# Routed experts: the last three of 39 token blocks put under a condition on the number of blocks the routing fills

## The chip, the cores and the metric

The kernel runs on one core of a Trainium2 chip. The metric is device time in microseconds (us) of that core, as the median of repeated runs; lower is better. One further execution was taken under the hardware profiler, and all views of a profile in this document come from such an execution.

A core has five engines with a queue of instructions each: TensorE (PE in the views; PEld is its weight load), VectorE (DVE), ScalarE (ACT), GpSimd (POOL) and SyncE (SP, which here issues most DMAs). A name with a q behind it (SPq, POOLq) means the sequencer of that engine: register, semaphore, branch and DMA-issuing instructions. Each engine works its own queue in order and waits on semaphores for the others.

## The reference, cut to what matters

Four layers act on x, of shape 32 x 128 x 256, each as `x = x + layer(layernorm(x))`: an attention over a context, a quantized feed-forward, a second attention, and a routed feed-forward with 8 experts. The change lies in the last one:

```python
def _L1_ffn_ref(x, W1, b1, W2, b2, Wr, br):
    E, D, H = (8, 256, 1024)
    routing_logits = x @ Wr + br
    indices = jnp.argmax(softmax(routing_logits), axis=-1)
    out = jnp.zeros_like(x)
    for i in range(E):
        mask = (indices == i).astype(x.dtype)[..., None]
        h = jax.nn.relu((x * mask) @ W1[i] + b1[i])
        out = out + (h @ W2[i] + b2[i])
    return out
```

Each of the 4096 tokens meets the two weight matrices of one expert only; what the seven others add for a masked row is a constant vector for each expert (`kacc` in the kernel).

## The kernel before

The first three layers, and the counting of the routing, are done by line 1480; the change does not touch them. While the second attention is finished, each token is given an expert and a slot, and its row (layer norm and residual side by side, 2 x 256 numbers) is written to `rows_d` in DRAM.

The expert stage follows. Tokens of one expert are cut into blocks of 128 rows. The number of blocks of an expert is its count divided by 128, rounded up, at least 1 (`nblk_f`, L1510); a running sum over the experts gives where each one ends (`endb`, L1512), so that its last entry is the number of blocks in use. Since the routing is not known when the program is built, the loop is written out for the most that 4096 tokens and 8 experts can need: `NB` = 39 blocks. A block `j` past the end takes the last expert (`eb` is cut at 7) and has row numbers out of range, so that its gather and its scatter move nothing; its arithmetic is done all the same.

The order of work is not that of `j`. The blocks are laid in `NW` = 3 parts, and turn `s` takes block `SEQ[s]`: the parts are worked in rotation, each with a set of weight buffers of its own (`w1s`, `w2s`, `kbs`, indexed by `s % NW`). So a new expert's weights are fetched into one set while the two other parts are at work. Whether a part changes expert at block `j` is the flag `new`, computed on the chip; SP loads flag and expert number into registers (L1598, L1599) and issues the three weight DMAs with the flag as condition (L1600, L1606, L1609). The first set is fetched much earlier, during the second attention.

For each turn `s`:

- `fetch(s)` (L1577, POOL): gather of the 128 rows by the token numbers `tok_i`, into one of `NX` = 4 buffers `xb`, issued three turns ahead;
- `turn(s)` (L1620 PE, L1622 DVE): the 128 x 256 block is transposed;
- `inner(s)` (L1633 PE, then L1642 ACT and L1646 DVE): 1024 hidden values, bias and relu;
- `outer(s)` (L1657 PE, L1653 and L1662 DVE): back to 256 values, and the constants and the residual added;
- scatter of the rows to the output (L1663, POOL), each one waiting for the one before it to have landed;
- `fetch_1(s + 3)` and `fetch_2(s + 3)` (SP): the weights of the turn that uses this set next.

In the loop PE and DVE keep the order in which the program is written (`manual_schedule`); a scheduler orders the other three. The loop runs `inner(s)`, `turn(s + 1)`, `outer(s)`, so PE has the next transposes and products in its queue while ACT and DVE finish the hidden values. After the last turn come the closing semaphores and drains (L1743).

Of the kernel before, what the change touches and what calls it, by code (L numbers as in the profile page):

```python
# [10 lines left out]
I32 = mybir.dt.int32  # L11
# [4 lines left out]
ALU = mybir.AluOpType  # L16
# [4 lines left out]
P = 128  # L21
# [15 lines left out]
def tile_xattn_ffn_d2(  # L37
# [25 lines left out]
    nc = tc.nc  # L63
    B, S, D = x.shape
# [8 lines left out]
    E = b2.shape[0]  # L73
# [3 lines left out]
    NB = (B * S - E) // P + E  # L77

    NW = 3
    NB = -(-NB // NW) * NW  # L80
    SEQ = [(s % NW) * (NB // NW) + s // NW for s in range(NB)]

    dram = ctx.enter_context(tc.tile_pool(name="dram", bufs=1, space=DRAM))
    x1_d = dram.tile([B, P, D], F32, name="x1_d")
# [109 lines left out]
    with (  # L194
# [35 lines left out]
        def whole(parts):  # L230
# [12 lines left out]
            out=bmask8, in_=bmask8, pattern=[[-HD0, hpc]], compare_op=ALU.is_ge,  # L243
# [3 lines left out]
            out=bmask8, in_=bmask8, pattern=[[HD0, hpc]], compare_op=ALU.is_ge,  # L247
# [98 lines left out]
        def turn(b):  # L346

            t = tiles[b]
            t["tr"] = ptr.tile([P, 4, P], F32, tag="tr", name="tr")
            for k in range(KD):  # L350
                ks = slice(k * P, (k + 1) * P)
                nc.tensor.transpose(t["tr"][:, k, :], t["xn"][:, ks], ident)
                nc.tensor.transpose(t["tr"][:, KD + k, :], of(b, "c")[:, ks], ident)
# [828 lines left out]
    with (  # L1182
# [77 lines left out]
        out=below, in_=ones, pattern=[[1, P]], compare_op=ALU.is_gt,  # L1260
# [19 lines left out]
    NP, NX = 1, 4  # L1280
    W1N = w1b.shape[1]
    w1s = [res.tile([P, W1N], F32, name=f"w1s{i}") for i in range(NP)]
    w2s = [res.tile([P, MF * D], F32, name=f"w2s{i}") for i in range(NP)]
    kbs = [res.tile([P, D], F32, name=f"kb{i}") for i in range(NP)]
    xbs = [res.tile([P, W], F32, name=f"xb{i}") for i in range(NX)]
# [42 lines left out]
    with tc.manual_schedule(engines=by_hand):  # L1328
# [15 lines left out]
        for n in range(N):  # L1344
# [117 lines left out]
            out=toks, in_=toks_d.rearrange("(k c p) o -> c k (p o)", p=P, c=P)  # L1462
# [19 lines left out]
    with (  # L1482
# [28 lines left out]
        endb = dr.tile([P, E], F32, name="endb")  # L1511
# [13 lines left out]
        for s in range(NW):  # L1525
            nc.vector.memset(new[:, SEQ[s] : SEQ[s] + 1], 1.0 if s else 0.0)

        plan1 = dr.tile([P, 2], I32, name="plan1")
        plan = dr.tile([P, 2, NB], I32, name="plan")
        for i, v in enumerate((eb, new)):  # L1530
            nc.vector.tensor_copy(plan1[:, i : i + 1], v[:, SEQ[1] : SEQ[1] + 1])

        def plan_others():
            for i, v in enumerate((eb, new)):
                nc.vector.tensor_copy(plan[:, i, :], v)
# [40 lines left out]
        def gather(dst, table, idx, bound):  # L1576
            nc.gpsimd.indirect_dma_start(  # L1577
                out=dst, out_offset=None, in_=table,
                in_offset=bass.IndirectOffsetOnAxis(ap=idx, axis=0),
                bounds_check=bound, oob_is_err=False,  # L1580
            )
# [3 lines left out]
        def fetch(s):  # L1585
            j = SEQ[s]
            gather(xbs[s % NX], rows_d, tok_i[:, j : j + 1], B * P - 1)

        exps_, news = {}, {}

        def fetch_1(s):

            j = SEQ[s]
            row = (
                [plan1[0:1, i : i + 1] for i in range(2)] if s == 1
                else [plan[0:1, i, j : j + 1] for i in range(2)]
            )
            exps_[s] = nc.sync.value_load(row[0], min_val=0, max_val=E - 1)  # L1598
            news[s] = nc.sync.value_load(row[1], min_val=0, max_val=1)  # L1599
            nc.sync.dma_start(  # L1600
                out=w1s[s % NW], in_=w1b[bass.ds(exps_[s] * P, P), :], cond=news[s] > 0
            )

        def fetch_2(s):
            e, new_ = exps_.pop(s), news.pop(s)
            nc.sync.dma_start(  # L1606
                out=w2s[s % NW], in_=w2[bass.ds(e * P, P), :], cond=new_ > 0
            )
            nc.sync.dma_start(  # L1609
                out=kbs[s % NW],  # L1610
                in_=kacc_d[bass.ds(e, 1), :].rearrange("e d -> (e d)").partition_broadcast(P),
                cond=new_ > 0,
            )
# [9 lines left out]
            return xbT  # L1623

        def inner(j, xbT):
            wb = w1s[j % NW]
            hT = wk_.tile([P, MF, P], F32, tag="hT", name="hT")
            for q in range(2):
                h_ps = ph.tile([P, 4, P], F32, tag="h", name="h_ps")
                for c4 in range(4):  # L1630
                    c = q * 4 + c4
                    for k in range(KD):
                        nc.tensor.matmul(  # L1633
                            h_ps[:, c4, :],
                            lhsT=wb[:, k * FF + c * P : k * FF + (c + 1) * P],
                            rhs=xbT[:, k, :], start=(k == 0), stop=(k == KD - 1),
                        )
                for c4 in range(4):
                    c = q * 4 + c4
                    b1c = wb[:, KD * FF + c : KD * FF + c + 1]  # L1640
                    if c4 < 2:
                        nc.scalar.activation(  # L1642
                            hT[:, c, :], h_ps[:, c4, :], AF.Relu, bias=b1c
                        )
                    else:
                        nc.vector.tensor_scalar(  # L1646
                            hT[:, c, :], h_ps[:, c4, :], b1c, 0.0, ALU.add, ALU.max
                        )
            return hT

        def outer(j, hT):
            xk = wk_.tile([P, D], F32, tag="xk", name="xk")
            nc.vector.tensor_tensor(xk, xbs[j % NX][:, :D], kbs[j % NW], ALU.add)  # L1653
            w2t = w2s[j % NW].rearrange("p (c d) -> p c d", d=D)
            y_ps = py.tile([P, 512], F32, tag="y", name="y_d")
            for c in range(MF):
                nc.tensor.matmul(  # L1657
                    y_ps[:, :D], lhsT=hT[:, c, :], rhs=w2t[:, c, :],
                    start=(c == 0), stop=(c == MF - 1),
                )  # L1660
            yb = wk_.tile([P, D], F32, tag="yb", name="yb")
            nc.vector.tensor_tensor(yb, y_ps[:, :D], xk, ALU.add)  # L1662
            nc.gpsimd.indirect_dma_start(  # L1663
                out=out_rows, out_offset=bass.IndirectOffsetOnAxis(
                    ap=tok_i[:, SEQ[j] : SEQ[j] + 1], axis=0
                ),
                in_=yb, in_offset=None, bounds_check=B * P - 1, oob_is_err=False,
            )


        with tc.manual_schedule(engines={mybir.EngineType.PE, mybir.EngineType.DVE}):
            for s in range(NX - 1):
                fetch(s)
            fetch_1(1)
            fetch_2(1)
            nxt = turn(0)
            plan_others()
            fetch_1(2)
            fetch_2(2)
            for s in range(NB):  # L1680
                hT = inner(s, nxt)
                if s + NW < NB:
                    fetch_1(s + NW)
                if s + 1 < NB:
                    nxt = turn(s + 1)
                if s + NX - 1 < NB:
                    fetch(s + NX - 1)
                outer(s, hT)
                if s + NW < NB:
                    fetch_2(s + NW)  # L1690


# [54 lines left out]
```

## Time and profile before

| | us |
|---|---|
| median of 3 runs | 1617.8 (1615.79 to 1618.09) |
| the profiled execution, its own time | 1616.39 |
| its span, first to last instruction | 1614.7 |
| busy PE / PEld | 1521.8 / 1132.9 |
| busy DVE / ACT / POOL | 950.5 / 809.0 / 461.1 |
| mean granted TensorE clock | 0.988 of full |
| products L1633 and L1657 of the 39 blocks, busy | 147.8 + 141.1 |
| first product of the expert stage, last scatter issued | 1318.58, 1604.00 |

Times of instructions are counted from the start of the span. A row of a group gives line, engine, operation, tiles and count, then busy time and the mean of one in ns, then idle time of the engine just before and what ended it. A row of one line of the source gives the durations of its instructions as min/median/max in ns, and when the first and the last began. A row of a stretch gives its length, the busy time of each engine with the number of instructions, the granted clock, the share of time in which the DMA engines were busy, and what they moved in GB/s.

### The profile page before, as it was taken

How to read it: one execution, taken by the hardware profiler on the slowest of the kernel's cores; microseconds unless marked ns; L12 is line 12 of the kernel's file. 1: busy time of each engine (PE TensorE's matmuls, PEld its weight loads, DVE VectorE, ACT ScalarE, POOL GpSimd, SP SyncE). 2: the span in 40 equal slices, each digit the busy share in tenths (PEclk: the TensorE clock that was granted, in tenths of full speed). 3: DMA queues.
4: the chain of work that ended last, by engine and by line, in shares of the span. 5: the costliest groups of instructions: out<-in, count | busy, mean ns of one | idle time of the engine just before them, and what ended most of it. 6: DMA issues, size and time to landing. Idle time of an engine off the chain costs nothing. (4 is left out here: it accounts for less than half of the span.)

```text
span 1614.7 us, 28238 instructions
## 1 busy us (share of the span) xinstructions
PE 1521.8 (94%) x10062; PEld 1132.9 (70%) x10062; DVE 950.5 (59%) x2275; ACT 809.0 (50%) x2421; POOL 461.1 (29%) x533
## 2 busy tenths in 40 slices
PE   7999998999988899999999999999999969999997
PEld 4665665544433588787777777777777649999996
DVE  6989896347999434465555566566655433333332
ACT  5787885447979432655555555554455401111111
POOL 6566663000000002233333333323332222232321
PEclk9999999999999999999999999999999979999998
DMA  7222211002438756122111110010000343134410
GB/s 230 86 67 77 69 38 50 0 33 85 160 148 263 239 184 229 36 49 84 56 55 53 53 53 27 27 27 21 9 14 14 92 164 105 53 105 160 154 35 8
DMA packets 83724, 137.76 MB, mean 85 GB/s; under 512 B 13034, under 2 KB 61053, under 8 KB 80256
## 3 DMA queue, kind: packets, MB, share of 16 engines
q1 hardware_dynamic: 73664, 122.92, 23.0%
q0 software_dynamic: 5952, 12.61, 2.5%
q8 instruction: 80, 1.31, 0.4%
q10 hardware_dynamic: 3968, 0.42, 0.2%
q14 instruction: 60, 0.49, 0.1%
HBM read 159.48 MB, written 46.16 MB: 127 GB/s over the span
## 5 line engine op out<-in xcount | busy, mean ns | idle before, releaser
L1021 ACT ACTIVATE pr_c<-sc_c,nmaxc 128x128 f32<-128x128 f32 x512 | 183.4, 389 | 277.3 <-DVE nmaxc L1012 167.4
L1033 POOL TENSOR_TENSOR pr_c<-pr_c,rsumc 128x512 f32<-128x512 f32 x64 | 93.0, 1452 | 321.6 <-DVE rsumc L1030 181.5
L1642 ACT ACTIVATE hT<-h_ps,w1s 128x128 f32<-128x128 f32 x156 | 48.7, 364 | 254.0 <-issue 175.8
L960 DVE TENSOR_SCALAR qT<-ps_qk,bqk 128x256 f32<-128x256 f32 x128 | 61.8, 484 | 176.0 <-ACT kT L956 176.0
L1633 PEld LDWEIGHTS h_ps<-xbT,w1s 128*128 128x128 f32 x1248 | 147.5, 194 | 2.9 <-DVE xbT L1622 0.9
L1633 PE MATMUL h_ps<-xbT,w1s 128*128 128x128 f32 x1248 | 147.8, 277 | 0.5 <-DVE xbT L1622 0.5
L404 ACT ACTIVATE pr<-sc_a,nmaxa 128x128 f32<-128x128 f32 x512 | 139.9, 401 | 4.9 <-DVE nmaxa L395 4.9
L1657 PE MATMUL y_d<-w2s,hT 128*128 128x256 f32 x624 | 141.1, 379 | 0.0
L950 PE MATMUL ps_qk<-rT,wq_s 128*128 128x256 f32 x512 | 132.3, 381 | 7.0 <-DVE rT L934 7.0
L950 PE MATMUL ps_qk<-cT,wk_s 128*128 128x256 f32 x512 | 138.5, 393 | 0.0
L1657 PEld LDWEIGHTS y_d<-w2s,hT 128*128 128x128 f32 x624 | 115.5, 190 | 14.1
L1646 DVE TENSOR_SCALAR hT<-h_ps,w1s 128x128 f32<-128x128 f32 x156 | 47.5, 346 | 127.3 <-ACT hT L1642 125.3
L1072 PE MATMUL y_ps<-wo_s,oT 128*128 128x256 f32 x512 | 117.1, 382 | 0.0
L1021 ACT ACTIVATION_READ_ACCUMULATOR pr_c<-sc_c,nmaxc 128x1 f32 x512 | 116.7, 228 | 0.0
L950 PEld LDWEIGHTS ps_qk<-rT,wq_s 128*128 128x128 f32 x512 | 96.5, 190 | 23.3 <-DVE rT L934 10.6
L1072 PEld LDWEIGHTS y_ps<-wo_s,oT 128*128 128x128 f32 x512 | 94.7, 190 | 12.2 <-DVE pid L1496 0.4
L950 PEld LDWEIGHTS ps_qk<-cT,wk_s 128*128 128x128 f32 x512 | 87.5, 190 | 15.7 <-issue 2.1
L395 DVE TENSOR_REDUCE nmaxa<-sc_a 128x4 f32<-128x512 f32 x128 | 82.2, 684 | 16.0 <-PE sc_a L386 14.7
L1577 POOL DMA_INDIRECT xb<-rows_d,tok_i x39 | 39.9, 1023 | 178.2 <-PE y_d L1657 166.1
L1215 PE MATMUL ps_dn<-wdT,oq 128*128 128x256 f32 x384 | 83.7, 380 | 6.0 <-ACT oq L1197 6.0
L663 PE MATMUL ps_vf<-wv_f,cf 128*128 128x512 f32 x160 | 74.8, 620 | 12.4 <-DMA cf<-ct_d 10.6
L1215 PEld LDWEIGHTS ps_dn<-wdT,oq 128*128 128x128 f32 x384 | 72.7, 190 | 17.0 <-ACT oq L1197 7.2
(266 smaller groups left out, 3034.5 us busy)
## 6 DMA issues: line engine op xcount, KB each, us to landing
w1s<-in_W1b_dram SPq DMA_DIRECT2D x39, 1028.0 KB
w2s<-in_W_dram SPq DMA_DIRECT2D x39, 1024.0 KB
v_d<-vs SPq DMA_DIRECT2D x40, 256.0 KB
v<-v_d SPq DMA_DIRECT2D x10, 1024.0 KB
u_d<-u SPq DMA_DIRECT2D x12, 768.0 KB
ub<-u_d SPq DMA_DIRECT2D x12, 768.0 KB
w2e<-in_W_dram SPq DMA_DIRECT2D x8, 1024.0 KB
rows_d<-row SPq DMA_DIRECT2D x32, 256.0 KB
```

The lines of the kernel that those rows point to most:

```text
L395: nc.vector.tensor_reduce(u["nmax"][:, r, :], u["scs"][r], AX.X, ALU.max, negate=True)
L404: nc.scalar.activation(u["pr"][:, r * HQ + j, :], u["scs"][r][:, j, :], AF.Exp, bias=u["nmax"][:, r, j : j + 1],)
L663: nc.tensor.matmul(ps, lhsT=cfs[b][:, k, :], rhs=wv_f[:, k, h * 512 : (h + 1) * 512], start=(k == 0), stop=(k == KD - 1),)
L950: nc.tensor.matmul(ps[:, j, :], lhsT=w_[:, k, m * P : (m + 1) * P], rhs=src[:, k, :], start=(k == 0), stop=(k == KD - 1),)
L960: nc.vector.tensor_scalar(s["qT"][:, m, :], ps[:, 1, :], bqk[:, 0, m : m + 1], HD1**-0.5, ALU.add, ALU.mult,)
L1021: nc.scalar.activation(u["pr"][:, h, :], u["scs"][par][:, mm, :], AF.Exp, bias=u["nmax"][par][:, mm : mm + 1], accum_out=u["sums"][:, h : ...
L1033: eng.tensor_tensor(pr[:, j : j + 4, :], pr[:, j : j + 4, :], bc(rsum[:, j : j + 4], 2, P), ALU.mult,)
L1072: nc.tensor.matmul(t["y_ps"][:, :D], lhsT=t["oT"][:, m, :], rhs=wo_s[:, m, :], start=(m == 0), stop=(m == M1 - 1),)
L1215: nc.tensor.matmul(ps[:, j, :], lhsT=oq[:, m, j * P : (j + 1) * P], rhs=wdT[:, m, :], start=(m == 0), stop=(m == M0 - 1),)
L1633: nc.tensor.matmul(h_ps[:, c4, :], lhsT=wb[:, k * FF + c * P : k * FF + (c + 1) * P], rhs=xbT[:, k, :], start=(k == 0), stop=(k == KD - 1),)
L1642: nc.scalar.activation(hT[:, c, :], h_ps[:, c4, :], AF.Relu, bias=b1c)
L1657: nc.tensor.matmul(y_ps[:, :D], lhsT=hT[:, c, :], rhs=w2t[:, c, :], start=(c == 0), stop=(c == MF - 1),)
```

## The change

The number of blocks in use, `endb[7]`, is written to `used_i` and loaded into a register of every engine (`used`). The loop now runs over `NM` = 36 turns, in three parts of twelve (blocks 0 to 11, 12 to 23, 24 to 35). The remaining three blocks, 36 to 38, are written out behind the loop, one inside the other, each under the condition that `used` is greater than its number; each does its own fetches, its transposes and its products, one after the other, with the weights in the third set (`buf`). So whichever blocks are not in use are jumped over.

```diff
     NB = -(-NB // NW) * NW
-    SEQ = [(s % NW) * (NB // NW) + s // NW for s in range(NB)]
+
+    NT1 = 3
+    NM = NB - NT1
+    SEQ = [(s % NW) * (NM // NW) + s // NW for s in range(NM)] + [*range(NM, NB)]
...
+        used_i = dr.tile([P, 1], I32, name="used_i")
+        nc.vector.tensor_copy(used_i, endb[:, E - 1 : E])
+
         def plan_others():
...
+        def buf(s):
+
+            return s % NW if s < NM else NW - 1
+
...
-                out=w1s[s % NW], in_=w1b[bass.ds(exps_[s] * P, P), :], cond=news[s] > 0
+                out=w1s[buf(s)], in_=w1b[bass.ds(exps_[s] * P, P), :], cond=news[s] > 0
...
-                out=w2s[s % NW], in_=w2[bass.ds(e * P, P), :], cond=new_ > 0
+                out=w2s[buf(s)], in_=w2[bass.ds(e * P, P), :], cond=new_ > 0
...
-            nc.vector.tensor_tensor(xk, xbs[j % NX][:, :D], kbs[j % NW], ALU.add)
-            w2t = w2s[j % NW].rearrange("p (c d) -> p c d", d=D)
+            nc.vector.tensor_tensor(xk, xbs[j % NX][:, :D], kbs[buf(j)], ALU.add)
+            w2t = w2s[buf(j)].rearrange("p (c d) -> p c d", d=D)
...
             plan_others()
+            used = nc.values_load(used_i[0:1, 0:1], min_val=1, max_val=NB)
             fetch_1(2)
             fetch_2(2)
-            for s in range(NB):
+            for s in range(NM):
                 hT = inner(s, nxt)
-                if s + NW < NB:
+                if s + NW < NM:
                     fetch_1(s + NW)
-                if s + 1 < NB:
+                if s + 1 < NM:
                     nxt = turn(s + 1)
-                if s + NX - 1 < NB:
+                if s + NX - 1 < NM:
                     fetch(s + NX - 1)
                 outer(s, hT)
-                if s + NW < NB:
+                if s + NW < NM:
                     fetch_2(s + NW)
+
+        def last(s):
+
+            with tc.If(used > s):
+                fetch(s)
+                fetch_1(s)
+                fetch_2(s)
+                outer(s, inner(s, turn(s)))
+                if s + 1 < NB:
+                    last(s + 1)
+
+        last(NM)
```

More of the change, by code (lines that the diff above doesn't have):

```diff
@@ L1606, in fetch_2 @@
             nc.sync.dma_start(
-                out=w2s[s % NW], in_=w2[bass.ds(e * P, P), :], cond=new_ > 0
+                out=w2s[buf(s)], in_=w2[bass.ds(e * P, P), :], cond=new_ > 0
             )
             nc.sync.dma_start(
-                out=kbs[s % NW],
+                out=kbs[buf(s)],
                 in_=kacc_d[bass.ds(e, 1), :].rearrange("e d -> (e d)").partition_broadcast(P),
@@ L1625, in inner @@
         def inner(j, xbT):
-            wb = w1s[j % NW]
+            wb = w1s[buf(j)]
             hT = wk_.tile([P, MF, P], F32, tag="hT", name="hT")
```

## The prediction

> **What bounds the kernel now.** I read the page first, then the expert stage in stretches, its waits, the SP queue for weight loads, and the closing line.
>
> ```profile
> PE 1521.8 (94%) x10062; PEld 1132.9 (70%) x10062; DVE 950.5 (59%) x2275; ACT 809.0 (50%) x2421; POOL 461.1 (29%) x533
> q0 software_dynamic: 5952, 12.61, 2.5%
> q8 instruction: 80, 1.31, 0.4%
> ```
>
> PE is busy 94% of the span. Queue q0 (POOL's gathers and scatters) moved 12.61 MB: 4096 rows of 2 KB in and of 1 KB out are 12.58 MB, so only real rows travel.
>
> From the expert stage's stretches (a cut inside the loop, two of 1 us during a weight load, then five scatters, turns 34 to 38):
>
> ```profile
> 1347.00:1362.00 15.00, 15.00 (x104) 14.12 (x103) 5.12 (x17) 2.50 (x8) 4.10 (x4) 1.00 0.17 54
> 1460.00:1461.00 1.00, 1.00 (x12) 1.00 (x11) 0.00 (x0) 0.55 (x2) 0.34 (x1) 1.00 1.03 411
> 1464.00:1465.00 1.00, 1.00 (x6) 0.89 (x5) 0.12 (x1) 0.00 (x0) 0.14 (x1) 1.00 0.66 236
> ...
> 1575.00:1580.00 5.00, 5.00 (x39) 4.79 (x38) 1.84 (x6) 1.25 (x4) 1.02 (x1) 1.00 0.08 26
> 1582.40:1587.00 4.60, 4.60 (x37) 4.42 (x36) 1.59 (x6) 1.25 (x4) 1.00 (x1) 1.00 0.01 2
> 1589.60:1594.00 4.40, 4.40 (x36) 4.25 (x35) 1.35 (x5) 1.25 (x4) 0.98 (x1) 1.00 0.08 30
> 1596.90:1601.00 4.10, 4.10 (x34) 3.95 (x33) 1.11 (x4) 1.25 (x4) 0.98 (x1) 1.00 0.03 8
> 1604.00:1608.00 4.00, 0.00 (x0) 0.00 (x0) 0.00 (x0) 0.00 (x0) 0.98 (x1) 0.78 0.01 0
> ```
>
> In the loop PE has no gap at full granted clock, and the waits show PE held once, for 0.5 us, after turn 0's transposes. A turn is as long as PE's work in it: turns repeat every 7.245 us (POOL's gathers at 1559.05, 1566.29, 1573.54). Turns 35 (block 37) and 38 (block 38) send nothing, 34 and 36 a full block (26 GB/s x 5 us = 130 KB), 37 a tail, yet PE works through all of them. So an empty block costs a whole turn.
>
> How many are empty? SP's weight issues tell. A DMA whose flag is set takes 0.34 us to issue, else 0.08:
>
> ```profile
> 1420.21 0.35 SPq L1600 DMA_DIRECT2D w1s<-in_W1b_dram  x1
> 1427.44 0.08 SPq L1600 DMA_DIRECT2D w1s<-in_W1b_dram  x1
> ...
> 1456.42 0.34 SPq L1600 DMA_DIRECT2D w1s<-in_W1b_dram  x1
> ```
>
> Turn 3's issue is at 1325.95 and one follows every 7.245 us, so these are turns 16, 17, 21. In all, the long ones are turns 4, 16, 21, 23, 28, 30: blocks 14, 18, 7, 33, 22, 10. The reference's routing, carried through for its inputs, gives 889, 298, 445, 406, 469, 414, 832, 343 tokens, hence 7, 3, 4, 4, 4, 4, 7, 3 blocks with ends at 7, 10, 14, 18, 22, 26, 33, 36: the same blocks (26 begins the third part, loaded without a flag). So 36 blocks are filled; 36, 37 and 38 are empty, and the first condition, `used > 36`, is false. The nearest count to a block's edge, 889, would need 8 more tokens.
>
> The closing line, and the register load that SP already does:
>
> ```profile
> L1743 SPq EVENT_SEMAPHORE  x12: 17/28/23572, 1582.4 to 1614.6; - x12
> L1743 POOLq DRAIN  x3: 46/107/10115, 1603.8 to 1614.4; - x3
> L1598 SPq TENSOR_LOAD <-plan x38: 262/268/483, 1305.8 to 1575.1; - x38
> L1598 SPq FUSED_REGOPS  x38: 164/164/183, 1306.3 to 1575.4; - x38
> L1598 SPq SEQ_ASSERT  x38: 18/18/28, 1306.6 to 1575.6; - x38
> ```
>
> The last scatter is issued at 1604.00, and SP sees it landed at 1582.4 + 23.6 = 1606.0. But POOL's drain, from 1603.8, lasts 10.1 us, to 1613.9, and the span ends at 1614.7. So POOL ends the tail, 10.7 us behind the last issue; PE, DVE, ACT and SP have 7 us and more to spare.
>
> **The change, part by part.**
>
> *Three turns fewer.* 3 x 7.245 = **-21.74 us**, all on PE's path. The new last turn ends as the old one did (no transposes for a next block). Its block 35 has 343 - 256 = 87 rows, so its scatter lands perhaps 0.4 us later than an empty one (landing 2.1 shortest, 2.5 median): hidden under POOL's drain.
>
> *used_i.* One cast on 128 x 1 on DVE, in the chain from the last count to `tok_i` for which POOL and PE wait. Two such casts (L1531) start 0.11 us apart: **+0.1**.
>
> *The register on five engines.* 0.27 + 0.16 + 0.02 = 0.45 us each by SP's rows. SP stands before turn 2's weights, whose flags it awaits until 1318.7 anyhow; ACT is idle 24.7 us there, DVE 4.4, POOL 13.3. PE's load stands between turn 0's transposes and `inner(0)`, a stretch of 1.2 us (1317.38 to 1318.58). All 0; without that cover 0.45 once.
>
> *Moved switches.* With parts of twelve, experts change at turns 7, 8, 19, 21, 29, 30, 31: seven loads for six, three of them in adjacent turns. Each is 1028 + 1024 + 128 KB. The trace's load issued at 1456.42 has its data through by 1464.8, at about 400 GB/s. A set's w1 is issued 16.2 us before its first product (turn 4: 1333.26, needed at 1327.8 + 3 x 7.245 = 1349.5), its w2 18 us. Three sets and three turns of gathers and scatters are 3 x (2.2 + 0.4) = 7.8 MB, 19.5 us at 400 GB/s, and the turns take 21.7; no queue builds up. Cost 0. Cover: each set's 8 us of slack, and 11 us for a gather (issued 1327.21, its transposes at 1338.7); if a set came later, PE would stand for exactly the excess. SP and POOL issue the same instructions per turn as before.
>
> *The condition.* The trace has no conditional jump. On PE, DVE, ACT and SP it has 7 us of cover. On POOL it stands before the drain. Lower bound 0: if the drain's 10 us run from the last scatter, whatever stands between lies inside them; and even -9, should the drain shrink because the scatter has landed before it starts. Upper bound 18.5: the landing (2.5), a code fetch (5.9, as long as the slowest scatter landing), and a second drain of 10.1 before the jump. I take **+3.2**: POOL awaits the last scatter (2.5), since the scatter in the skipped part follows it, as L1663 does in the loop; compare and jump 0.1; some 20 semaphore instructions of 28 ns, to make up for what the skipped part would have signalled.
>
> [...]
>
> *Sum:* -21.74 + 0.1 + 3.2 = **-18.4 us**. Against the profiled execution's own time, 1616.4, that is 1598.0; the median stands 1.4 above it, so **1599.4**.
>
> **The rivals.**
>
> *A costly join (0.15).* The condition waits for all engines and drains POOL on its own account: 3.2 to 18.5 becomes the price, the gain 4 to 15, midpoint about 10: 1608. For it: POOL's 10 us drain at the end shows what such a thing can cost. Against: a second drain with nothing new queued should be short (the others of that row took 0.05 and 0.1).
>
> *A cheaper tail (0.03).* The drain shrinks: gain 22 to 30, some 1592. Nothing shows what it waits for after 1606.0.
>
> *The jump is not taken (0.02), slower.* If `used` were larger, the blocks behind the loop run unpipelined: turn 0, issued at 1308.95, had its `yb` at 1328.6, 19.7 us, against 7.245 in the loop. One entered block gives -21.7 + 19.7 + 3.2 = +1, about no change; from the second on it is slower, +21 or 1639. The counts speak against it.
>
> *The loop's turn grows (0.08), slower.* Some wait of the conditional program, or weights arriving late after all, in each turn. It eats the gain at 18.4 / 36 = 0.51 us a turn and is slower beyond; 0.8 gives +10, 1628. Against: the loop's instructions are the same, and PE's queue decides.
>
> **How the numbers follow.** The main case has 0.70: gain 15 to 22, 1595 to 1603. Price of exactly the saving: 0.02. Faster 0.70 + 0.15 + 0.03 = 0.88, same (within 0.2%, 3 us, about what a measurement can tell from no change) 0.02, slower 0.10. The range 1594 to 1607 leaves out the costliest part of the join (0.05), half of the cheap tail (0.015), and the last 0.12.
>
> **What would show it.** L1633 with 1152 products for 1248, 36 gathers and scatters; turns still 7.245 us with PE at 1.00 in the stretches of turns 26 to 31; last scatter near 1582.4; POOL's closing drain, and its distance to the end (10.7 before, 13.9 by my sum). A last scatter later than 1583 refutes the loop's part, a tail beyond 16 us the condition's; a POOL queue with its branch and a second long drain is the costly join.

## The result, and the profile after

The changed kernel takes 1596.17 us (median of 5 runs, 1592.13 to 1598.08), the kernel before 1617.97 us beside it. The ratio is 0.9863, with a 95% interval of 0.9847 to 0.9879. The forecast was 1599.4 us with a range of 1594 to 1607: the time lies in the range, and the gain, 21.8 us, is somewhat more than the 18.4 us forecast. The profiled executions differ less, by 20.0 us (1616.39 against 1596.36), and so do their spans.

From the page of the changed kernel, the engines and the queue of POOL's gathers and scatters:

```profile
PE 1501.1 (94%) x9912; PEld 1112.6 (70%) x9912; DVE 943.8 (59%) x2255; ACT 806.4 (51%) x2409; POOL 455.1 (29%) x527
q0 software_dynamic: 5568, 12.61, 2.5%
```

PE has 150 products fewer, 50 for each of three turns, and its busy time is 20.7 us shorter. POOL's queue moves the same 12.61 MB in fewer packets. So all the rows still travel, and the three blocks that are gone carried none.

The products of the hidden values before (L1633) and after (L1643), SP's weight issues of turns 29 to 31, and the stretches in which these three turns' weights arrive (the columns are as before: length, PE, PEld, DVE, ACT and POOL busy with counts, granted clock, DMA share, GB/s):

```profile
L1633 PE MATMUL h_ps<-xbT,w1s 128*128 128x128 f32 x1248 | 147.8, 277 | 0.5 <-DVE xbT L1622 0.5
```

```profile
L1643 PE MATMUL h_ps<-xbT,w1s 128*128 128x128 f32 x1152 | 135.9, 277 | 0.7 <-DMA kb<-kacc_d 0.7
```

```profile
1514.45 0.35 SPq L1610 DMA_DIRECT2D w1s<-in_W1b_dram  x1
...
1521.37 0.33 SPq L1610 DMA_DIRECT2D w1s<-in_W1b_dram  x1
...
1528.62 0.33 SPq L1610 DMA_DIRECT2D w1s<-in_W1b_dram  x1
```

```profile
1514.50:1521.70 7.20, 7.20 (x52) 6.79 (x51) 2.26 (x8) 1.25 (x4) 2.04 (x2) 1.00 0.86 315
1521.70:1529.00 7.30, 7.30 (x52) 6.89 (x51) 2.36 (x8) 1.25 (x4) 2.04 (x2) 1.00 0.86 293
1529.00:1536.20 7.20, 7.20 (x52) 6.79 (x51) 2.26 (x8) 1.25 (x4) 2.05 (x2) 1.00 0.99 362
```

1152 products for 1248 are 36 turns. SP's long issues in the loop stand at turns 7, 8, 19, 21, 29, 30 and 31, the seven that the prediction named. In the stretches of the last three the DMA engines are busy for 86 to 99% of 22 us, and PE has no gap.

The tail, from two views: the last scatter in the timeline, and the instructions of the line of the condition (L1705), of the register load (L1688) and of the closing line (L1766), which was L1743 before (durations min/median/max in ns, first and last start):

```profile
1581.31 0.42 DVE L1672 TENSOR_TENSOR yb<-y_d,xk 128x256 f32<-128x256 f32 x1 [1.85 <-PE y_d L1667]
1582.01 0.98 POOL L1673 DMA_INDIRECT out_dram<-yb,tok_i  x1 [6.04 <-DVEq L1705]
```

```profile
L1688 POOLq TENSOR_LOAD <-used_i x1: 509/509/509, 1582.1 to 1582.1; - x1
...
L1705 POOLq EVENT_SEMAPHORE  x3: 17/43/43, 1582.9 to 1583.0; - x3
...
L1705 PEldq COMPARE_BRANCH  x1: 393/393/393, 1579.2 to 1579.2; - x1
...
L1705 DVEq COMPARE_BRANCH  x1: 72/72/72, 1581.3 to 1581.3; - x1
L1705 DVEq EVENT_SEMAPHORE  x1: 21/21/21, 1581.9 to 1581.9; - x1
L1705 POOLq COMPARE_BRANCH  x1: 57/57/57, 1582.7 to 1582.7; - x1
L1705 POOLq INC_SWDGE_SEM  x1: 2248/2248/2248, 1583.1 to 1583.1; - x1
...
L1766 POOLq DRAIN  x3: 46/107/8404, 1585.4 to 1594.4; - x3
```

Behind the issue of the last scatter POOL loads the register, jumps, spends 2.25 us in INC_SWDGE_SEM, and begins its closing drain, which ends at 1585.4 + 8.4 = 1593.8. The tail is 12.7 us, against 10.7 before.

**A yardstick.** The first gather is issued anywhere between 1306.9 and 1317.8 us in the executions shown below, although hardly anything ahead of it was changed (the small cast; in `if_early` also the place of register loads). What the change does lies behind that point. I therefore compare traces from the first gather's issue (all times from POOL's timeline; the stretch to the last scatter, the tail from there to the span's end, and their sum, in us):

| kernel | first gather | to last scatter | tail | sum |
|---|---|---|---|---|
| before | 1308.95 | 295.05 | 10.70 | 305.75 |
| changed | 1309.11 | 272.90 | 12.69 | 285.59 |
| `no_cond` | 1313.31 | 272.73 | 10.16 | 282.89 |
| `twelve_39` | 1311.97 | 294.76 | 10.67 | 305.43 |
| `arm_one` | 1317.79 | 272.91 | 12.50 | 285.41 |
| `enter_one` | 1308.59 | 288.38 | 12.03 | 300.41 |
| `enter_three` | 1309.77 | 316.50 | 10.73 | 327.23 |
| `no_last_scatters` | 1309.15 | 258.60 | 15.45 | 274.05 |
| `all_new` | 1312.68 | 272.49 | 12.63 | 285.12 |
| `if_before_last` | 1306.87 | 274.06 | 10.27 | 284.33 |
| `if_early` | 1311.47 | 273.90 | 10.23 | 284.13 |

By this measure the change gains 20.16 us: 22.15 up to the last scatter, less 2.0 in the tail.

The yardstick has a spread of its own, in turn 0. From the first gather to the one for turn 4, which waits for turn 0's last products, it takes 17.4 to 18.3 us in these executions (18.26 before, 17.84 after). PE comes out of its wait for the first rows at a granted clock of 0.50 and is at 1.00 by 1325 us; between 1318 and 1325 us the mean is 0.64 before and 0.72 after. The 32 products of turn 0, before and after:

```profile
1318.58 5.92 PE L1633 MATMUL h_ps<-xbT,w1s 128*128 128x128 f32 x32 [0.52 <-DVE xbT L1622]
```

```profile
1319.05 5.19 PE L1643 MATMUL h_ps<-xbT,w1s 128*128 128x128 f32 x32 [0.71 <-DMA kb<-kacc_d]
```

So differences of a few tenths of a us between sums are not read as effects of an edit.

### The profile page after: what moved, and what is told of

Its sections match the earlier page's. It is cut to its first block, busy times and chain, and to the rows that moved or that the text cites. A ratio compares the mean times of both kernels' runs of the same rounds, so it can differ in the third digit from the quotient of the medians.

```text
span 1594.7 us, 27850 instructions
## 1 busy us (share of the span) xinstructions
PE 1501.1 (94%) x9912; PEld 1112.6 (70%) x9912; DVE 943.8 (59%) x2255; ACT 806.4 (51%) x2409; POOL 455.1 (29%) x527
## 3 DMA queue, kind: packets, MB, share of 16 engines
q0 software_dynamic: 5568, 12.61, 2.5%
## 5 line engine op out<-in xcount | busy, mean ns | idle before, releaser
L1652 ACT ACTIVATE hT<-h_ps,w1s 128x128 f32<-128x128 f32 x144 | 45.1, 364 | 235.7 <-issue 161.1
L1643 PEld LDWEIGHTS h_ps<-xbT,w1s 128*128 128x128 f32 x1152 | 135.6, 194 | 2.9 <-DVE plan L1541 1.1
L1643 PE MATMUL h_ps<-xbT,w1s 128*128 128x128 f32 x1152 | 135.9, 277 | 0.7 <-DMA kb<-kacc_d 0.7
L1667 PE MATMUL y_d<-w2s,hT 128*128 128x256 f32 x576 | 130.3, 379 | 0.0
L1667 PEld LDWEIGHTS y_d<-w2s,hT 128*128 128x128 f32 x576 | 106.6, 190 | 13.0
L1656 DVE TENSOR_SCALAR hT<-h_ps,w1s 128x128 f32<-128x128 f32 x144 | 43.9, 347 | 117.2 <-ACT hT L1652 117.2
L398 DVE TENSOR_REDUCE nmaxa<-sc_a 128x4 f32<-128x512 f32 x128 | 82.3, 685 | 14.4 <-PE sc_a L389 13.2
L666 PE MATMUL ps_vf<-wv_f,cf 128*128 128x512 f32 x160 | 75.0, 620 | 12.7 <-DMA cf<-ct_d 10.8
L1005 PE MATMUL sc_c<-kT,qT 64*128 64x128 f32 x1024 | 79.8, 288 | 6.0 <-ACT pr_c L1024 6.0
L1015 DVE TENSOR_REDUCE nmaxc<-sc_c 128x4 f32<-128x512 f32 x128 | 81.9, 682 | 4.5 <-PE sc_c L1005 4.3
```

Of the source, the lines that this page charges most:

```text
L398: nc.vector.tensor_reduce(u["nmax"][:, r, :], u["scs"][r], AX.X, ALU.max, negate=True)
L666: nc.tensor.matmul(ps, lhsT=cfs[b][:, k, :], rhs=wv_f[:, k, h * 512 : (h + 1) * 512], start=(k == 0), stop=(k == KD - 1),)
L1005: nc.tensor.matmul(scs[par][:, mm, :], lhsT=s["qT"][half, m, tok], rhs=s["kT"][half, m, tok], start=True, stop=True,)
L1015: nc.vector.tensor_reduce(nmax, u["scs"][par], AX.X, ALU.max, negate=True)
L1643: nc.tensor.matmul(h_ps[:, c4, :], lhsT=wb[:, k * FF + c * P : k * FF + (c + 1) * P], rhs=xbT[:, k, :], start=(k == 0), stop=(k == KD - 1),)
L1667: nc.tensor.matmul(y_ps[:, :D], lhsT=hT[:, c, :], rhs=w2t[:, c, :], start=(c == 0), stop=(c == MF - 1),)
```

## The experiments

Theory: the gain is PE's time in three empty turns, the new order is free, and the condition costs some 2 us in the tail, on POOL. The rivals are named in each run's expectation.

**The condition taken out (`no_cond`).** What it costs.

```diff
-        used_i = dr.tile([P, 1], I32, name="used_i")
-        nc.vector.tensor_copy(used_i, endb[:, E - 1 : E])
...
-            used = nc.values_load(used_i[0:1, 0:1], min_val=1, max_val=NB)
...
-        last(NM)
```

> The 36 turns of the changed kernel, with the register `used`, its cast and the three conditional blocks taken out: blocks 36 to 38 are never computed. My theory: the saving is the PE time of three empty turns, and the condition gives 2.0 us of it back in the tail (12.7 us from the last scatter's issue to the end of the span, against 10.7 before). So here: turns of 7.245 us, last scatter near 1582, tail 10.7, span about 2.2 us under the changed kernel's, 1592 to 1593; gain over the kernel before near 24 us. Rival A (the condition is free, the tail is longer because the last scatter now carries rows instead of none): tail stays at 12.7, span 1594.5. Rival B (a third of the saving comes from elsewhere, the program being smaller): the last scatter moves by over 1 us against the changed kernel's 1582.0.

The turn is 7.245 us, as before. The tail is 10.16 us and the sum 282.89. The closing line of this kernel (L1762):

```profile
L1762 POOLq DRAIN  x3: 46/107/9627, 1585.8 to 1596.0; - x3
```

So the condition costs 2.5 us of tail. The sums differ by 2.7; the other 0.2 is turn 0 (17.84 against 17.68), within its spread. Rival A falls, since the last scatter carries rows here too; rival B falls, since the stretch to the last scatter is within 0.2 us of the changed kernel's. The timed runs do not show it: ratio 0.9867 (0.9843 to 0.9891), beside 0.9863 for the changed kernel.

**The order alone (`twelve_39`).**

```diff
-            for s in range(NM):
+            for s in range(NB):
                 hT = inner(s, nxt)
...
-                if s + 1 < NM:
+                if s + 1 < NB:
                     nxt = turn(s + 1)
-                if s + NX - 1 < NM:
+                if s + NX - 1 < NB:
                     fetch(s + NX - 1)
...
-        last(NM)
```

(The cast and the register load are taken out as above.)

> The new order alone: parts of twelve, the last three blocks as turns 36 to 38 at the end of the same pipelined loop, no condition; their weight issues are left out, which these inputs do not need. My theory: the order costs nothing, since seven loads are covered as six were; the time is the kernel before's within 0.2%: span 1614.7 +- 2, tail 10.7 (last scatter empty again), gain 0. Rival (the order itself helps or hurts, for instance the weights of turns 29 to 31 late, or a lighter start without the load of turn 4): off by 2 us or more, with PE waiting in those turns or the first product of turn 1 earlier.

The sum is 305.43 us against 305.75, and the ratio to the kernel before 1.0007 (0.9993 to 1.0021). The new order neither helps nor hurts, to within 0.2% of the time. With `no_cond`, which differs from it by the three turns alone, it settles the gain: 22.03 us to the last scatter for three turns of 7.245 (21.74), and the last 0.3 us is turn 0 (17.97 against 17.68).

**One block in the conditional part (`arm_one`).** What sets POOL's 2.25 us.

```diff
                 outer(s, inner(s, turn(s)))
-                if s + 1 < NB:
-                    last(s + 1)
```

> The changed kernel with one conditional block in place of three nested ones (blocks 37 and 38 are never computed). The jumped-over part then holds 2 of POOL's DMAs, not 6. In the changed kernel POOL spends 2.25 us in one instruction that makes up for the semaphores of the DMAs jumped over (INC_SWDGE_SEM). If that price is for each DMA, it falls to about 0.75 us and the tail from 12.7 to 11.2 us. If it waits for the last scatter to be worked off or landed, it stays at 2.2 and the tail at 12.6.

```profile
L1705 POOLq INC_SWDGE_SEM  x1: 2236/2236/2236, 1591.6 to 1591.6; - x1
```

2.24 us for two DMAs jumped over, as for six. It is not a price for each DMA. Nor does it end with a landing: in `enter_one`, where four are jumped over, it takes 2.26 us and begins only 0.1 us behind the last scatter's issue, against 1.1 us in the changed kernel (that scatter was of an empty block). In these runs it takes 2.22 to 2.26 us. What POOL does in it stays open: that it makes up for semaphores is read from its name and place and shown by no trace, and the INC_SWDGE_SEM at the start of the program takes 0.03 us. (This kernel's one run took 1604.87 us; its late first gather, 1317.79, accounts for that, and its sum is the changed kernel's within 0.2 us.)

**One and three blocks entered (`enter_one`, `enter_three`).** The prediction's slower rival, priced.

```diff
-            with tc.If(used > s):
+            with tc.If(used > (s - 1 if s == NM else s)):
```

```diff
-            with tc.If(used > s):
+            with tc.If(used > s - NT1):
```

> The changed kernel with the first condition loosened by one, `used > 35`, so that the (empty) block 36 is entered and the next condition, one level in, is false. It prices an entered block. By the prediction's rival: 19.7 us from fetch to yb less the cold start of turn 0 (2 us), so 17 to 20 us over the changed kernel: span near 1612 to 1614, about the kernel before's. Theory of a cheap entry (gather of an empty block moves nothing, so no 8 us for it): 12 to 14 us, span 1607. Theory of a costly entry (all engines meet, code is fetched): over 22 us, slower than before.

> The changed kernel with all three conditions loosened by three, so that the three (empty) blocks are entered one inside the other. One entered block cost 14.8 us (300.4 against 285.6 us from the first gather's issue to the end). If each entered block costs the same, since nothing of one overlaps the next, the stretch is 285.6 + 3 x 14.8 = 330 us, or 2 us less without the jump's price: 24 us over the kernel before's 305.7, a time near 1641, slower by 1.4%. If later ones are cheaper, because the gathers and weight steps of a nested block run ahead on POOL and SP while PE works the one before, the step falls toward 7 to 10 us a block: 308 to 318 us, 1620 to 1630.

The timeline of the entered block of `enter_one`, and two stretches of it:

```profile
1581.48 0.98 POOL L1673 DMA_INDIRECT out_dram<-yb,tok_i  x1 [6.04 <-DVE yb L1672]
1583.08 1.05 POOL L1583 DMA_INDIRECT xb<-rows_d,tok_i  x1 [0.61 <-issue]
...
1585.36 0.66 PE L1630 MATMUL tr_d<-ident,xb 128*128 128x128 f32 x2 [4.62 <-DMA xb<-rows_d,tok_i]
...
1586.53 6.24 PE L1643 MATMUL h_ps<-xbT,w1s 128*128 128x128 f32 x32 [0.52 <-DVE xbT L1632]
...
1596.97 1.00 POOL L1673 DMA_INDIRECT out_dram<-yb,tok_i  x1 [12.85 <-DVEq L1705]
```

```profile
1574.00:1581.00 7.00, 6.74 (x46) 5.97 (x44) 1.95 (x7) 1.25 (x4) 0.98 (x1) 1.00 0.05 19
1586.00:1593.00 7.00, 6.48 (x35) 6.44 (x35) 1.37 (x4) 0.81 (x3) 0.00 (x0) 0.60 0.00 0
```

And the products of the three entered blocks of `enter_three`:

```profile
1587.66 6.11 PE L1643 MATMUL h_ps<-xbT,w1s 128*128 128x128 f32 x32 [0.52 <-DVE xbT L1632]
...
1602.72 5.44 PE L1643 MATMUL h_ps<-xbT,w1s 128*128 128x128 f32 x32 [0.52 <-DVE xbT L1632]
...
1616.88 5.20 PE L1643 MATMUL h_ps<-xbT,w1s 128*128 128x128 f32 x32 [0.52 <-DVE xbT L1632]
```

One entered block adds 14.8 us to the sum, between the two forecasts of 12 to 14 and 17 to 20. Three add 41.6, to 327.2, where the expectation had 328 for blocks that do not overlap and a jump that is not paid (`enter_three` jumps over nothing and has no INC_SWDGE_SEM). Between scatters an entered block takes 15.5 us in `enter_one`, and 15.4, 14.4 and 13.9 us in `enter_three`. The dear part is seen in the rows: the gather is issued only behind the last scatter, PE waits 4.6 us for it, and then works at a granted clock of 0.60, so that the 32 products take 6.24 us for 3.73 in the loop. In the later blocks of `enter_three` they take 5.44 and 5.20 us, which is most of what those blocks are cheaper by. With one block entered the kernel is still faster than before, 0.9967 (0.9955 to 0.9979); with three it is slower, 1.0139 (1.0109 to 1.0170). The theory of a costly entry falls, and so does that of later blocks at 7 to 10 us. The blocks entered here are empty: one with rows has a real gather to wait for and may cost more; that was not run.

**The last scatters left out (`no_last_scatters`).** Why the tail is over 10 us.

```diff
+            if j >= NM - 2:
+                nc.vector.tensor_copy(kept[:, j - NM + 2, :], yb)
+                return
             nc.gpsimd.indirect_dma_start(
```

(On top of `no_cond`.)

> The 36 turns without the condition, and without the scatters of turns 34 and 35 (their rows are kept in SBUF and never reach the output). Theory: POOL's closing drain ends 8.4 us after POOL's last software DMA, whatever the rest of the core does, and that is why the tail is 10.2 to 12.7 us. POOL's last DMA is then turn 33's scatter, some 14.5 us before the last product ends, so the drain is over before PE is: the span ends about 1 us after the last DVE instruction, 9 to 10 us sooner than without this edit, near 272.5 us after the first gather's issue (282.9 before the edit). Rival: the 8.4 us is a closing step that POOL makes after all engines are done (or that runs from its own start): the end stays some 8 us behind the last DVE instruction.

```profile
1567.75 0.98 POOL L1675 DMA_INDIRECT out_dram<-yb,tok_i  x1 [6.24 <-DVE yb L1671]
...
1581.78 0.29 DVE L1673 COPY kept<-yb 128x256 f32<-128x256 f32 x1
```

```profile
L1766 POOLq DRAIN  x3: 46/107/9462, 1567.5 to 1582.9; - x3
```

The drain ends at 1567.5 + 9.46 = 1577.0, 8.2 us behind the end of POOL's last scatter (1568.73), while PE and DVE are still at work; the span ends at 1583.2, 1.1 us behind DVE's last instruction. The sum falls by 8.8 us, a little under the 9 to 10 forecast. The rival, a closing step after all engines are done, falls. POOL's drain ends 8.2 to 8.4 us behind the end of its last software DMA, or of INC_SWDGE_SEM where that comes last, and 8.7 to 8.9 us where the last scatter is an empty one (before, `twelve_39`, `enter_one`, `enter_three`). What it waits for is not shown: in every one of these kernels that DMA, or INC_SWDGE_SEM, is also POOL's last work, so that a wait for something that the DMA leaves behind and a fixed length from POOL's last work on are not told apart. The drain before the first DMA, at the start of the program, takes 0.19 us. The half microsecond more behind an empty scatter is why the tail before was longer than that of `no_cond`.

**Every turn loads its weights (`all_new`).** The cover of the moved switches.

```diff
+        nc.vector.memset(new[:, 1:NM], 1.0)
```

> The changed kernel with the flag `new` set for every turn after the first, so that each of the 36 turns loads its expert's 2.2 MB afresh, 36 loads for 9. It tests the term put at nothing, that adjacent switches are covered: 2.2 + 0.4 MB a turn at the 400 GB/s that the trace reaches is 6.5 us, under the 7.245 of a turn. Theory: no queue builds up, PE shows no gap, the turn stays at 7.25 us; time within 0.3% of the changed kernel's. Rival: sustained, the DMA engines give less (the three adjacent loads ran at 362 GB/s with a busy share of 0.99, which would be 7.2 us a turn, just at the edge), gathers come late, and the turn grows to 7.5 us or more: plus 9 us or more.

```profile
1430.00:1460.00 30.00, 30.00 (x206) 28.25 (x205) 10.03 (x31) 5.02 (x16) 8.20 (x8) 1.00 0.98 365
1460.00:1490.00 30.00, 30.00 (x206) 28.22 (x206) 9.23 (x28) 5.02 (x16) 8.70 (x9) 1.00 0.98 355
```

With 35 loads in the stage for 9 the DMA engines are busy 97 to 99% of the time and PE has no gap; the turn stays 7.245 us, the sum is 285.12. The theory holds, though with hardly any room to be seen: the engines move 350 to 365 GB/s, which is what the turns ask for (2.63 MB in 7.245 us are 363 GB/s), and they are busy nearly the whole turn with it. Whether they could sustain 400 is not shown. The rival was right on the rate and wrong on the consequence.

**The condition ahead of the last turn (`if_before_last`), and the register loaded early (`if_early`).**

```diff
-    SEQ = [(s % NW) * (NM // NW) + s // NW for s in range(NM)] + [*range(NM, NB)]
+    PART = (0, 2, 1)
+    SEQ = [PART[s % NW] * (NM // NW) + s // NW for s in range(NM)] + [*range(NM, NB)]
...
-            return s % NW if s < NM else NW - 1
+            return s % NW if s < NM else 1
...
             for s in range(NM):
+                if s == NM - 1:
+                    last(NM)
                 hT = inner(s, nxt)
...
-        last(NM)
```

(The last turn's `xbT` has a buffer of its own. In `if_early` the `values_load` stands ahead of the first `fetch`.)

> The changed kernel with the conditional blocks moved from behind the last turn to before it (the parts are rotated 0, 2, 1, so that the third part, whose weight set the conditional blocks share, has its last block in turn 34). POOL's steps for the condition (register load 0.5, branch, 2.25 us for the semaphores) then lie in the 6 us for which it waits for the last turn's rows. Theory: the tail returns from 12.7 to 10.2 us; PE pays a break between turns 34 and 35 for its branch (0.2 to 0.4 us) and the last transposes' copy, 0.4 to 1.5 us in all; from the first gather's issue to the end 284 to 285 us against 285.6, a gain of 1 us, too little for the timed runs. Rival: at the condition each engine meets all the others, and PE, which was a turn ahead of POOL, stands for POOL's 2.25 us and the scatter before it: 4 us or more lost at PE, 288 us or more.

> As the one before, and the register load of `used` moved ahead of the first gathers. In the changed kernel PE's load (0.49 us) came after turn 0's transposes and held the first product by about 0.2 us. Theory: PE loads while it waits 9 us for the gather, and turn 0 is 0.2 us shorter (from the first gather's issue to the fourth's 17.7 us, not 17.85); ACT's and POOL's loads move too, or not, to no effect. Rival: POOL's load now stands before its first gather and delays it by 0.5 us, and with it everything.

The last turn of `if_before_last` in its timeline, and from the line of the condition:

```profile
1572.89 0.98 POOL L1674 DMA_INDIRECT out_dram<-yb,tok_i  x1 [6.26 <-DVEq L1694]
1572.92 3.81 PE L1644 MATMUL h_ps<-xbT,w1s 128*128 128x128 f32 x32 [0.77 <-DVEq L1694]
...
1580.93 0.98 POOL L1674 DMA_INDIRECT out_dram<-yb,tok_i  x1 [7.05 <-DVE yb L1673]
```

```profile
L1694 DVEq COMPARE_BRANCH  x1: 72/72/72, 1572.2 to 1572.2; - x1
L1694 DVEq EVENT_SEMAPHORE  x1: 21/21/21, 1572.8 to 1572.8; - x1
...
L1694 POOLq INC_SWDGE_SEM  x1: 2223/2223/2223, 1574.0 to 1574.0; - x1
```

INC_SWDGE_SEM now lies at 1574.0 to 1576.2, while POOL waits for rows, and the tail is back to 10.27 us. PE stands 0.77 us until DVE, behind the rows of turn 34, has passed the condition too (DVEq L1694); 0.5 us of that lies between the end of DVE's branch and its next instruction. The stretch to the last scatter is 1.16 us longer. The net is 1.26 us in the trace's sum. PE met DVE there but did not wait for POOL's 2.2 us, so the rival falls. In `if_early` PE and DVE load early, while ACT's and POOL's loads stay at the condition, so its rival was not put to the test. PE's first product waits 0.52 us again, for 0.71, and turn 0 takes 17.84 us against 17.99, the sum 284.13 against 284.33: of the size forecast, and within turn 0's spread, so that a gain is not shown. The timed runs do not tell these two from the changed kernel: 0.9865 (0.9840 to 0.9890) and 0.9876 (0.9853 to 0.9899), so that I claim no better version by time.

## Why the prediction was right, step by step

- *Three turns fewer, -21.74.* Right: 22.15 us between the two traces, of which 0.4 is turn 0 at its rising clock, which varies from execution to execution. The last scatter came at 1582.01, forecast near 1582.4. That blocks 36 to 38 are empty, read from the flagged issues and the routing, is borne out: they were jumped over, and their absence changed no byte of POOL's traffic.
- *`used_i`, +0.1.* The cast is there, at 1303.82, and DVE's next instruction starts 0.06 us later. Too small to be told by the end.
- *The register, 0.* The load takes 0.46 to 0.54 us on each engine. PE's stood between the transposes and the first product, as expected, and was not all covered: the product waited 0.2 us longer, less than turn 0 varies by. POOL's was ordered behind the last scatter's issue, not early as I had it: by the order of its rows some half a microsecond on the tail, a term that the sum lacked. No run moved it alone.
- *Moved switches, 0.* Right, and shown with nearly four times the loads. The working's 400 GB/s was a peak; the rate seen over 30 us is 350 to 365. The cover of a gather was misread: the one issued at 1327.21 is turn 4's, whose transposes begin at 1346.0, so that it has 18.8 us, not 11 (1338.7 belongs to turn 3). The slip is on the safe side.
- *The condition, +3.2.* The size is near (2.0 against the tail before, 2.5 against `no_cond`), the make-up is wrong, and that the two are so near is luck: a landing of 2.5 us that does not count was put in the place of an instruction of 2.25 us that was not foreseen. POOL does not wait for the last scatter to land: it has jumped by 1582.8, 0.8 us after that scatter's issue, and no scatter of this kernel landed in under 2.3. In its place stand the register load and INC_SWDGE_SEM, 2.25 us. No run shows the 0.1 us that my sum took for compare and jump: the branch takes 0.05 to 0.07 us on SP, ACT, DVE and POOL in the changed kernel, and 0.39 on PE.
- *The code fetch.* The 5.9 us for it in the upper bound were an allowance of mine; that a jump here fetches code is not shown. Behind the taken branch POOL's next instruction follows within 0.2 us; no stall is seen on the path. On DVE the next instruction came 0.5 us behind its branch, off the path in this kernel and on it in `if_before_last`; what DVE does in that time is not shown.
- *The base.* I put the forecast 1.4 us above the sum, since the median stood above the profiled execution. After, the two agree within 0.2 us. That 1.4, the condition's 1.2 too many and turn 0's 0.4 add up to 3.0 of the 3.2 us between forecast and time. Single executions differ by several us (1592.13 to 1598.08), and a fit as close as this is in part chance.

The costly join did not occur: the changed kernel has no second long drain on POOL. The rival of an entered block named its mechanism rightly, and its threshold, the second block, lies between the one and the three that were run; but at 19.7 us a block it was too dear by 5. The price was taken from turn 0, where the transposes began 8.4 us behind the gather's issue; in `enter_one` it is 2.3 us. Turn 0's gather had rows to bring and shared DMA engines that were 88% busy; the empty one had no rows and found them 6% busy, and the two causes were not separated.

## What to carry to other kernels

When a loop is written out for the worst case, look in the trace for the turns that move no bytes: each costs what its bound engine takes, here 7.245 us of PE. A condition behind the loop is worth its price only for blocks that are rarely in use, since what is inside it loses the pipeline: about 14 us for an empty block that costs 7 in the loop, so that by an estimate from these numbers (285.6 us and twice 14 against 305.75) two in use would turn the gain into a loss. Before pricing what is added at the end of a kernel, see which engine's closing steps end last; what lies on the others there may be covered, as the 0.39 us of PE's branch were here.

## What the runs showed of the hardware

- In these kernels POOL's closing drain lasts 8.2 to 8.4 us past the end of its last software DMA or INC_SWDGE_SEM (8.7 to 8.9 when the last scatter moved nothing), also while PE and DVE are still at work. With a scatter as the last act it was paid in full; without the last two scatters it was hidden whole.
- In these kernels the jumped path of a condition around POOL's DMAs costs POOL one INC_SWDGE_SEM of 2.22 to 2.26 us, for two, four or six DMAs alike. Placed where POOL waits for rows anyhow, it no longer lengthens the tail (10.27 us, against 10.16 without a condition).
- After 4.6 us of waiting PE's next 7 us had a mean granted clock of 0.60, and its 32 products took 6.24 us for 3.73, so that this break cost more than the wait itself. After the 0.77 us of `if_before_last` they took 3.81.
